# Moving slot distances from ScalarE to GpSimd, and one more layer-1 bias from TensorE to ScalarE, in a graph-network kernel

## The chip, the cores and the metric

One core of one Trainium2 chip. The metric is device microseconds of one execution. Engines are called as in the profile: PE is TensorE, PEld its weight loads, DVE is VectorE, ACT is ScalarE, POOL is GpSimd.

## The reference

A message-passing layer on 128 graphs of 64 nodes with 128 features. Every adjacent pair of nodes goes through a three-layer perceptron with a layernorm after each of the first two layers; the messages are summed per node, and an update perceptron of the same form follows.

```python
f_i = broadcast(part_feats[:, :, None, :]); f_j = broadcast(part_feats[:, None, :, :])
messages = _mlp(concatenate([f_i, f_j], -1), msg_w0, ... msg_b2)    # relu, LN, relu, LN, linear
messages = messages * coupling_matrix[..., None]
agg = sum(messages, axis=2)
updated = part_feats + _mlp(concatenate([part_feats, agg], -1), upd_w0, ... upd_b2)
```

The adjacency is sparse (about 1 in 8 and the diagonal), so the kernel computes only the edges that exist.

## The kernel before

Edges are packed into slots, 640 for each graph, so 1280 for a pair of graphs. Two pairs make a quad, with 5 chunks of 512 edges; four pairs make a block, with ten chunks. There are 160 chunks in 16 blocks. A loop over chunks issues work by a hand-made plan: `at(n, place, f, ...)` puts a call into iteration n at one of the places "a", "m", "b", "k", "x", "e" and some more. The plan fixes the order of instructions on every engine. Layer 1 of a chunk runs 8 iterations (L1) after its layer 0.

```python
def place(b):                       # where a block's edges lie among the slots, on POOL
    before = adp.tile([P, PB], F32, name="before")
    nc.gpsimd.tensor_tensor(before, cum, blk["deg"], op=ALU.subtract)
    blk["mid"] = adp.tile([P, PB], F32, name="mid")
    nc.gpsimd.tensor_tensor(blk["mid"], cum, before, op=ALU.add)
    ...
def distance(p):                    # ACT: distance of every slot from the middle of each node's slots
    D[p] = tpp.tile([P, CAP], F16, name="d", bufs=2)
    nc.scalar.activation(D[p], slot, AF.Abs, bias=blocks[b]["mid"][:, q:q + 1], scale=-1.0)

def make_tp(p):                     # DVE: 1 where the slot belongs to the node
    ...
    nc.vector.tensor_scalar(tp, D.pop(p), blocks[b]["deg"][:, q:q + 1], None, op0=ALU.is_lt)
...
def seed(n):                        # ACT puts the scaled bias into the PSUM bank of layer 1
    ...
    for t in range(CH):
        nc.scalar.activation(Z[n][:, t, :], W["b1b"], AF.Copy, scale=SR[q][:, k:k + 1])

def layer1(n):
    ...
    if n not in SEEDED:             # otherwise PE does it, with one matmul of 512 columns
        nc.tensor.matmul(ps, lhsT=SD[q], rhs=W["b1t"][:, CH * c:CH * c + CH, :], start=True, ...)
    for t in range(CH):
        nc.tensor.matmul(ps[:, t, :], lhsT=h[:, t * P:(t + 1) * P], rhs=W["w1c"], ...)
    nc.scalar.activation(Y[n], ps, AF.Relu)
...
for n in range(2, NCHK - L1):       # seven of ten chunks get the bias from ACT
    if n % CPB in (0, 1, 2, 6, 7, 9) or (n > CPB and n % CPB == 5):
        at(n + L1 - 2, "x", seed, n)
```

The bias has to be scaled by the layernorm's root of each edge. POOL computes the variance of a quad, ACT takes the root and splits it (sh), PE turns it (`ma<-ident,sh`), and ACT copies it out (sdT) for the bias matmuls of PE. For a chunk, the bias costs either PE one matmul or ACT four small copies.

## Time and profile before

| | before |
|---|---|
| median of 3 executions | 574.55 us (572.53 to 574.66) |
| span of the profiled execution | 569.1 us |
| start of the first layer 1 | 33.2 us |
| start of layer 1 of blocks 1, 2, 14, 15 (counted from 0) | 61.0, 92.6, 484.5, 520.0 us |
| one block in the middle | 32.65 us |
| bias: chunks by ACT, by PE | 104, 56 |

The block starts are read from the order of time on PE, as the start of the first layer-1 matmul of chunks 10, 20 and so on. In the text "interval 7" is the time from layer 1 of a chunk with number 7 in its block to layer 1 of the next one. The bias matmul of chunk 8, if it has one, lies at the end of interval 7. A block's length is the sum of the ten median intervals.

Two more views of the kernel before matter later. First, what PE's weight loads waited for from 200 to 500 us (total us, times, longest us):

```profile
PEld z L605 <- issue: 2.7, 16, 0.2
...
PEld hT L544 <- DVE st L548: 1.8, 8, 0.2
PEld z L605 <- ACT z L593: 0.3, 2, 0.2
```

No wait is longer than 0.2 us (the view leaves out waits of up to 0.15 us). Second, ACT's order of time in intervals 7 and 8 (start, duration, engine, line, operation, tiles):

```profile
245.64 0.70 ACT L538 ACTIVATE h<-hps,b0c 128x512 f32<-128x512 f32 x1
246.42 0.59 ACT L741 COPY ysumT<-ma 128x512 f32<-128x512 f32 x1
246.91 0.83 ACT L478 ACTIVATE d<-slot,mid 128x640 f16<-128x640 f16 x1
247.64 0.30 ACT L269 ACTIVATE m_sq<-m_v,eps_c 128x20 f32<-128x20 f32 x1
```

Remember the order: the copy of ysumT, which gives PE its PSUM bank "ma" back, comes straight after the relu h, and one of the distances stands behind it.

### The profile page before, as it was taken

The numbers are of one execution on the slowest core, as the hardware profiler recorded it, in microseconds if no ns is written. First come the engines' busy times: TensorE is split into PE (matmuls) and PEld (weight loads), VectorE is DVE, ScalarE is ACT, GpSimd is POOL, SyncE is SP. The second block draws the span as 40 slices with busy tenths as digits, with TensorE's granted clock in tenths as the row PEclk, the third lists the DMA queues.
The fourth block names the chain that finished last, engine by engine and source line by source line (L and its number), as shares of the span: only waits on it lengthen the run. The fifth ranks groups of instructions, "written<-read, shape, count | busy, mean of one in ns | idle before, by whom it ended". The sixth has DMA issues, their size and how long they took to land. (4 is left out here: it accounts for less than half of the span.)

```text
span 569.1 us, 15800 instructions
## 1 busy us (share of the span) xinstructions
PE 547.2 (96%) x5325; PEld 513.5 (90%) x5325; DVE 483.0 (85%) x1944; ACT 481.2 (85%) x1153; POOL 353.2 (62%) x911
## 2 busy tenths in 40 slices
PE   8799899999999999999999999999999999989894
PEld 7597889999999999999999999999999999979883
DVE  6768788998979899898989899898989989886685
ACT  6778989998989899898989899898989989885534
POOL 3535466766757676675758676675767666545452
PEclk9999999999999999999999999999999999999998
DMA  4475647354654745654556545647554545452101
GB/s 102 112 149 123 126 114 135 84 133 112 120 138 113 143 98 147 109 121 113 126 137 117 143 97 132 113 106 152 119 137 84 135 111 106 114 94 29 39 20 42
DMA packets 90770, 63.23 MB, mean 111 GB/s; under 512 B 57398, under 2 KB 74812, under 8 KB 90684
## 3 DMA queue, kind: packets, MB, share of 16 engines
q1 hardware_dynamic: 90396, 62.03, 49.8%
q8 instruction: 44, 0.72, 0.6%
q14 instruction: 42, 0.34, 0.2%
q10 hardware_dynamic: 288, 0.13, 0.1%
HBM read 6.82 MB, written 4.19 MB: 19 GB/s over the span
## 5 line engine op out<-in xcount | busy, mean ns | idle before, releaser
L605 PE MATMUL z<-w1c,h 128*128 128x128 f32 x1280 | 172.8, 278 | 0.0
L605 PEld LDWEIGHTS z<-w1c,h 128*128 128x128 f32 x1280 | 161.2, 192 | 7.7 <-issue 4.6
L548 DVE BATCH_NORM_STATS2 st<-hT 128x6 f32<-128x128 f32 x640 | 140.8, 281 | 30.3 <-PE hT L544 30.2
L593 ACT ACTIVATE z<-b1b,m_sd 128x128 f32<-128x128 f32 x416 | 154.3, 371 | 10.1
L615 DVE BATCH_NORM_STATS2 st<-y 128x6 f32<-128x128 f32 x640 | 137.3, 275 | 2.7 <-POOL m_d L245 1.3
L608 ACT ACTIVATE y<-z 128x512 f32<-128x512 f32 x160 | 94.4, 591 | 22.5 <-PE z L605 20.8
L538 ACT ACTIVATE h<-hps,b0c 128x512 f32<-128x512 f32 x160 | 109.5, 685 | 1.7 <-PE hps L535 1.6
L544 PE MATMUL hT<-ident,h 128*128 128x128 f32 x640 | 97.1, 274 | 1.8 <-DVE st L548 1.6
L678 POOL TENSOR_TENSOR w<-oh,m_q 128x320 f32<-128x320 f16 x126 | 92.1, 744 | 9.9 <-PE hT L544 5.3
L535 PE MATMUL hps<-s,abl 128*128 128x512 f32 (+3 forms) x256 | 91.8, 370 | 2.5 <-ACT h L538 2.0
L544 PEld LDWEIGHTS hT<-ident,h 128*128 128x128 f32 x640 | 74.7, 140 | 13.8 <-DVE st L548 4.6
L535 PE MATMUL hps<-s,abh 128*128 128x512 f32 (+3 forms) x256 | 78.3, 324 | 0.0
L691 PE MATMUL ys<-y,w 128*64 128x128 f32 x1280 | 76.9, 275 | 0.0
L691 PEld LDWEIGHTS ys<-y,w 128*64 128x64 f32 x1280 | 69.2, 137 | 4.2 <-issue 3.6
L245 POOL TENSOR_TENSOR m_d<-st 128x20 f32<-128x20 f32 x62 | 16.4, 264 | 80.6 <-DVE st L548 69.0
L517 DVE TENSOR_TENSOR j<-mk,cmpt 128x320 fp32r<-128x320 f32 x124 | 58.4, 471 | 1.2 <-PE mk L509 1.2
L493 POOL CAST i<-tp 128x640 fp32r<-128x640 f16 x58 | 41.7, 719 | 23.3 <-DVE tp L484 7.4
L478 ACT ACTIVATE d<-slot,mid 128x640 f16<-128x640 f16 x64 | 52.7, 824 | 0.0
L535 PEld LDWEIGHTS hps<-s,abl 128*128 128x128 f32 x256 | 49.1, 192 | 3.7 <-ACT h L538 2.7
L535 PEld LDWEIGHTS hps<-s,abh 128*128 128x128 f32 x256 | 49.2, 192 | 0.0
L469 DVE TENSOR_TENSOR abl<-mu,abh 128x512 fp32r<-128x512 f32 (+1 forms) x33 | 22.0, 667 | 30.3 <-ACT abh L463 30.2
L509 PE MATMUL mk<-tp,posall 128*128 128x320 f16 x126 | 37.7, 299 | 0.0
(227 smaller groups left out, 980.4 us busy)
## 6 DMA issues: line engine op xcount, KB each, us to landing
s<-i SPq DMA_DIRECT2D x124, 160.0 KB, 2.6
s<-j SPq DMA_DIRECT2D x124, 160.0 KB, 2.6
xn<-in_x_dram SPq DMA_DIRECT2D x15, 256.0 KB, 3.7
out_dram<-uo SPq DMA_DIRECT2D x15, 256.0 KB, 2.4
an<-in_adj_dram SPq DMA_DIRECT2D x16, 128.0 KB, 2.7
oh<-tp SPq DMA_TRANSPOSE x64, 3.3
xn<-in_x_dram SPq DMA_DIRECT2D x2, 128.0 KB
out_dram<-uo SPq DMA_DIRECT2D x2, 128.0 KB, 2.6
```

What stands on the lines that cost most here:

```text
L478: nc.scalar.activation(D[p], slot, AF.Abs, bias=blocks[b]["mid"][:, q:q + 1], scale=-1.0)
L517: nc.vector.tensor_tensor(JR[p][:, c], MK.pop((p, k))[:, 0:HC], cmpt[:, c], op=ALU.is_equal)
L535: nc.tensor.matmul(ps[:, c:c + w], lhsT=ab[:, g % 4, :], rhs=s, start=(k == 0), stop=(k == 1))
L538: nc.scalar.activation(H[n], ps, AF.Relu, bias=b0c)
L544: nc.tensor.transpose(ps[:, t, :], H[n][:, t * P:(t + 1) * P], ident)
L548: nc.vector.bn_stats(ST0[q][:, CH * c + t, :], ps[:, t, :])
L593: nc.scalar.activation(Z[n][:, t, :], W["b1b"], AF.Copy, scale=SR[q][:, k:k + 1])
L605: nc.tensor.matmul(ps[:, t, :], lhsT=h[:, t * P:(t + 1) * P], rhs=W["w1c"], start=False, stop=True, skip_group_check=True)
L608: nc.scalar.activation(Y[n], ps, AF.Relu)
L615: nc.vector.bn_stats(ST1[q][:, CH * c + t, :], Y[n][:, t, :])
L678: (nc.vector if p == NP - 2 else nc.gpsimd).tensor_tensor(WT[p][:, :, g, :], OH[p][:, :, g * N:(g + 1) * N], Q[q][:, k:k + TG].unsqueeze(2 ...
L691: nc.tensor.matmul(YS[b][g * N:(g + 1) * N, k, :], lhsT=w[:, t, g, :], rhs=y, start=(t == 0), stop=(t == TG - 1))
```

## The change

The intent is to use POOL, which is the least busy engine, for the distances, and to spend the ACT time that this frees on an eighth bias in ten, so that PE has less to do. On POOL the distance is a linear map, slot x scale + shift, written as a 16-bit float whose steps at 1536 are 1, so that the slots of a node all round to 1536 exactly; the comparison becomes "equal to 1536". Block 0 keeps ACT. Besides, the start is reordered: the bias table and the variance of the first quad change places, the second half of the first row terms goes to another PSUM bank, and nine small matmuls (keep_busy) are added to PE's work in the start.

```diff
@@ place(b)
-            blk["mid"] = adp.tile([P, PB], F32, name="mid")
-            nc.gpsimd.tensor_tensor(blk["mid"], cum, before, op=ALU.add)
+            half = adp.tile([P, PB], F32, name="half")
+            nc.vector.tensor_scalar(half, blk["deg"], 0.5, 2.0, op0=ALU.max, op1=ALU.mult)
+            blk["scale"] = adp.tile([P, PB], F32, name="scale")
+            nc.vector.reciprocal(blk["scale"], half)
+            mid = adp.tile([P, PB], F32, name="mid")
+            nc.gpsimd.tensor_tensor(mid, cum, before, op=ALU.add)
+            nc.gpsimd.tensor_tensor(mid, mid, blk["scale"], op=ALU.mult)
+            blk["shift"] = adp.tile([P, PB], F32, name="shift")
+            nc.gpsimd.tensor_scalar(blk["shift"], mid, -1.0, TIE, op0=ALU.mult, op1=ALU.add)
@@ rows(b, half)
-            ps = blk["ab_ps", half] if k0 else ubank()
+            ps = blk["ab_ps", half] if k0 else abank() if (b, half) == (0, 1) else ubank()
@@ distance(p), for b > 0
-            nc.scalar.activation(D[p], slot, AF.Abs, bias=blocks[b]["mid"][:, q:q + 1], scale=-1.0)
+            nc.gpsimd.tensor_scalar(D[p], slot, blocks[b]["scale"][:, q:q + 1],
+                                    blocks[b]["shift"][:, q:q + 1], op0=ALU.mult, op1=ALU.add)
@@ make_tp(p), for b > 0
-            nc.vector.tensor_scalar(tp, D.pop(p), blocks[b]["deg"][:, q:q + 1], None, op0=ALU.is_lt)
+                nc.vector.tensor_scalar(tp, D.pop(p), TIE, None, op0=ALU.is_equal)
@@ plan
-                    at(max(n - 7, p - 2), "a", distance, p)
+                    at(max(n - 7, p - 2), "x" if p == PB + 1 else "a", distance, p)
-                at(n - 5, "a", node_rows, p)
+                at(n - 5, "x" if p == PB else "a", node_rows, p)
-            at(n, "e0", var0_of, q)
+            at(3 if q == 0 else n, "x" if q == 0 else "e0", var0_of, q)
-            if n % CPB in (0, 1, 2, 6, 7, 9) or (n > CPB and n % CPB == 5):
+            if n % CPB in (0, 1, 2, 6, 7, 9) or (n > CPB and n % CPB in (5, 8)):
                 at(n + L1 - 2, "x", seed, n)
-        at(3, "b", bias_table)
+        at(3, "e", bias_table)
+        for n, k in ((2, 2), (3, 3), (4, 2), (5, 2)):
+            at(n, "e", keep_busy, k)
```

## The prediction

> **What bounds the kernel now.** I read the page first for the engines' shares, then the table of stretches, the order of time on TensorE (PE), the waits of PE, and last the groups and the order of time on GpSimd (POOL).
>
> ```profile
> PE 547.2 (96%) x5325; PEld 513.5 (90%) x5325; DVE 483.0 (85%) x1944; ACT 481.2 (85%) x1153; POOL 353.2 (62%) x911
> ```
>
> ```profile
> core 0: us, PE busy (x) PEld busy (x) DVE busy (x) ACT busy (x) POOL busy (x), PEclk, DMA share, GB/s
> 20.00:40.00 20.00, 17.00 (x136) 14.48 (x136) 13.36 (x46) 14.87 (x40) 11.12 (x18) 1.00 0.72 152
> ...
> 200.00:250.00 50.00, 50.00 (x500) 47.60 (x499) 45.56 (x188) 45.50 (x108) 34.34 (x92) 1.00 0.55 122
> 250.00:300.00 50.00, 50.00 (x502) 47.80 (x502) 44.07 (x178) 44.70 (x109) 33.23 (x84) 1.00 0.50 124
> ```
>
> The average hides three stages. From about 65 to 500 us PE never stops; ACT and DVE are busy about 90%, POOL 68%. In the first 65 us and the last 65 us PE has holes. A busy PE need not be one at its limit, because matmuls overlap and their ends are modelled, so I looked for a second sign: the same instruction one block (ten chunks of 512 edges) later. The turn of the layer-0 roots (L568) starts at 203.64 and again at 236.29, so a block takes 32.65 us; from the starts of layer 1 over thirteen blocks, nearly every chunk repeats within 0.02 us from block to block. An engine that waited on others would not repeat like that. So the middle is bound by what PE is given to do: 14 blocks x 32.65 = 457 us of the 569.
>
> The order of time on PE shows what one bias matmul (L602) costs. Columns: start, duration, engine, line, operation, operands, shapes, count.
>
> ```profile
> 213.14 0.60 PE L736 MATMUL ma<-ident,ysum 128*128 128x128 f32 x4
> 213.58 1.06 PE L605 MATMUL z<-w1c,h 128*128 128x128 f32 x8
> ...
> 215.51 0.60 PE L736 MATMUL ma<-ident,uy 128*128 128x128 f32 x4
> 215.87 0.48 PE L602 MATMUL z<-b1t,sdT 80*128 80x512 f32 x1
> 216.18 1.05 PE L605 MATMUL z<-w1c,h 128*128 128x128 f32 x8
> ```
>
> The same four transposes stand ahead of layer 1 twice: without the bias matmul layer 1 starts 0.44 us after them, with it 0.67 us. It costs 0.23 us of PE's stream, not its 0.48 us of duration.
>
> The start is another matter. The waits of PE in the first 70 us:
>
> ```profile
> PE ma L568 <- POOL sh L563: 2.3, 2, 1.5
> PE hps L535 <- ACT h L538: 2.0, 2, 1.6
> PE mu L180 <- DVE abl L469: 1.4, 1, 1.4
> ```
>
> The reader sees 5.7 us in which PE stood, of which 1.4 us come from a PSUM bank that the second half of the row terms held, and 1.6 us from ScalarE (ACT) reaching a relu late.
>
> **What the Trainium skill says.** "VectorE: DVE Perf Modes", section on the TRN2 errata, gives a matmul max(60, 6 + columns) cycles at 2.4 GHz: 518 cycles, 216 ns for 512 columns. The 0.23 us above agree. "ScalarE: Activation LUTs", section "What ACT_TABLE_LOAD costs", gives an ACTIVATE with a pointer operand 280 ns + 0.833 ns per element: 813 ns for 640 (the trace: 826) and 387 ns for 128 (the trace: 371). "GPSIMD Engine Reference", section 4.1, calls one-input operations on GpSimd roughly line-rate[...]; the cast below agrees (719 ns for 640), the tensor_scalar with a pointer doesn't obviously (about 620 ns for 128). "SBUF — State Buffer", section "Who interferes with whom", says that a VectorE (DVE) operation in a two-port mode and a GpSimd operation block each other whole; the trace agrees, since the slot comparison (L484) takes 0.36 us in most cases and about 1.01 us once in four, when a GpSimd operation runs.
>
> **The change part by part.** The groups that carry the costs:
>
> ```profile
> L478 ACT ACTIVATE d<-slot,mid 128x640 f16<-128x640 f16 x64 | 52.7, 824 | 0.0
> L593 ACT ACTIVATE z<-b1b,m_sd 128x128 f32<-128x128 f32 x416 | 154.3, 371 | 10.1
> L493 POOL CAST i<-tp 128x640 fp32r<-128x640 f16 x58 | 41.7, 719 | 23.3 <-DVE tp L484 7.4 <-ACT y L608 7.0 <-POOL posall L393 6.0
> L602 PE MATMUL z<-b1t,sdT 80*128 80x512 f32 x56 | 27.2, 486 | 0.0
> L646 POOL TENSOR_SCALAR b1lo<-b1lo,part 128x128 f32<-128x128 f32 x1 | 0.6, 622 | 0.1
> ```
>
> The two instruction orders, set against each other, give the counts.
>
> *Distances.* 60 of 64 leave ACT and become GpSimd tensor_scalars with two operations and two pointers. ACT loses 60 x 0.824 = 49.4 us, 3.3 us a block. What one costs on GpSimd is the weakest number here. At the cast's rate it is 0.72 us. The one tensor_scalar with a pointer in the trace took 0.62 us for 128 elements; if all above a fixed 0.2 us (operations of 4 elements take that) is per element, 640 take 2.3 us; if the excess is fixed, 1.04. I choose 1.3 us. GpSimd then gets 4 x 1.3 + 0.4 (two 4-element operations) = 5.6 us a block on top of 22.1 (67.6 us in 100 us, over the 32.65): 27.7 of 32.4, 85%. It isn't the bound. DVE gets two small operations a block, some 0.3 us.
>
> *Bias by ACT.* 14 bias matmuls go, 56 ACT copies of 0.371 come: 1.5 us more a block on ACT. With the distances gone ACT falls from 29.5 us a block to 29.5 - 3.3 + 1.5 = 27.7. PE saves 14 x 0.23 = 3.2 us, and in the middle all of it is on the path: the block should become 32.42 us. ACT's relief itself buys nothing there, because PE hardly waits for ACT.
>
> *Start.* The second half of the row terms takes another bank, and the first variance goes ahead of four table operations (0.46 + 0.62 + 0.62 + 0.45 = 2.2 us on GpSimd), in whose shadow ACT stood 1.8 us before the root. A distance (1.3 us) now stands there instead, so the variance gains about 0.9 us, and ACT is also rid of a cast (moved) and a distance ahead of the late relu: 0.7 + 0.8 us. Against that, nine warming matmuls of about 0.22 us enter PE, 2.0 us in all, placed in the holes. The bank's wait of 1.4 us shrinks to 0.7, since the next layer-0 matmul needs the same row terms anyway. The relu's 1.6 us should go. But the distance of the sixth pair now comes behind the first table part on GpSimd, at about 28.8 us, and its comparison on DVE can't run before that: DVE's next statistics start hardly earlier than the 29.55 us of before. I count 1.0 us of gain.
>
> Sum: 574.55 - 3.2 - 1.0 = 570.3 us. The end (500 us on) is not touched.
>
> **The rivals.**
>
> *GpSimd becomes a link that PE waits for.* The variance of a quad runs on GpSimd, goes to ACT, comes back and is turned by PE. GpSimd's slack ahead of it:
>
> ```profile
> 233.76 0.25 POOL L245 TENSOR_TENSOR m_d<-st 128x20 f32<-128x20 f32 x1 [1.78 <-DVE st L548]
> ...
> 249.19 0.25 POOL L245 TENSOR_TENSOR m_d<-st 128x20 f32<-128x20 f32 x1 [2.56 <-DVE st L548]
> ```
>
> One distance falls into the first gap, two into the second, where GpSimd works through from 233.76 to 246.6 with half a microsecond of rest. At 1.3 us each (2.6 in 2.56) they just fit. At 1.8 us the second variance is 1.0 us late, and PE's turn of the roots, which has at most 0.4 us of slack, waits perhaps 0.5 us a block: 14 x 0.5 = 7 us, about 577 us. At 2.3 us GpSimd has 31.6 of 32.4 us a block to do and each gap is missed: 1 us or more a block, 584 us or more. For it: the 622 ns of the lone tensor_scalar. Against: the cast's 719 ns for the same 640 elements.
>
> *The start gives more.* If the relu's wait goes and nothing catches up, 2 to 3 us instead of 1.0, and with 3.2 in the middle 568 us. If ACT's relief also removes the waits for the roots (2.3 us), 566. Against: those stand behind GpSimd, not ACT.
>
> *Nothing at the start, or a loss.* The warming matmuls (2.0 us) fill holes that no longer exist, and the late comparison holds DVE: 571 to 573 us.
>
> *Collisions.* Four more GpSimd operations a block meet DVE's two-port comparisons. A comparison lengthened by 0.65 us costs DVE up to 2.6 us of its 3 us of slack a block. The distance stands one chunk ahead of its own comparison, so few should meet; I give it no more than 0.5 us on average, inside the range.
>
> **Range and chances.** The certain term is 3.2 us of PE work; the others reach from +3 to -7 us or so. I take 570.3 us, 565.5 to 576.5. Over 2% faster needs 563.1 us or less, 11.5 us, when the visible removable PE time is 3.2 + 5.7: 0.03. Over 2% slower needs 586 us, which only the slowest GpSimd case gives: 0.04. Within: 0.93.
>
> **What would show it.** Right: 42 bias matmuls in place of 56; a block of 32.42 us with chunks repeating as exactly as before; PE busy throughout from 65 to 500; the distance at 1.0 to 1.5 us on GpSimd, GpSimd near 80% in the middle; ACT near 85%; layer 1 starting about 1 us before its 33.2 us of now. Wrong: a distance of 1.8 us or more with PE waiting for sh (L563's successor), or DVE waiting for d ahead of the comparison; a block of 32.65 us or longer; or a start shorter by 2 us or more.

## The result and the profile after

The changed kernel is slower: 581.59 us in the median of 4 executions (579.91 to 583.24), the kernel before 573.54 in the same rounds (570.91 to 574.66). A ratio here is the mean time of one kernel's runs over that of the other's of the same rounds, so not quite the ratio of the medians: 1.0147, interval 1.0098 to 1.0196. That is 1.5% slower, and above the range of the prediction (565.5 to 576.5), though in the class within 2% that it favoured; it had expected 0.7% less time, so the sign was wrong. The profiled spans are 569.1 and 579.5 us.

From the page after, engines and granted clock in 40 slices:

```profile
PE 554.1 (96%) x5329; PEld 513.5 (89%) x5329; DVE 487.0 (84%) x1974; ACT 458.0 (79%) x1149; POOL 410.8 (71%) x1001
...
PEclk9989999999999999999999999999999999998998
```

PE is busy for 6.9 us longer although it has less to do, ACT has lost 23 us and POOL gained 58. The groups after (busy us, mean ns):

```profile
L612 ACT ACTIVATE z<-b1b,m_sd 128x128 f32<-128x128 f32 x472 | 175.4, 372 | 11.5
...
L493 POOL TENSOR_SCALAR d<-slot,scale,shift 128x640 f16<-128x640 f16 x60 | 58.0, 966 | 0.1
```

The 56 new copies (472 for 416) and the 60 distances are there. A distance takes 0.97 us on POOL, less than the 1.3 us predicted, so the strongest rival of the prediction, a POOL that is too slow, is not the cause by itself. The table of stretches after:

```profile
20.00:40.00 20.00, 16.79 (x126) 14.57 (x125) 9.91 (x33) 10.24 (x29) 13.85 (x23) 0.91 0.61 127
...
200.00:250.00 50.00, 49.86 (x507) 46.58 (x502) 43.51 (x179) 40.59 (x103) 38.94 (x94) 1.00 0.60 114
```

Two things differ from before. In the first row the granted clock is 0.91 for 1.00, and DVE and ACT do a quarter to a third less. In the middle PE is no longer full, and ACT rests more.

**Where the 10.4 us went.** From the starts of layer 1:

| | before | after | difference |
|---|---|---|---|
| first layer 1 | 33.2 | 35.1 | +1.9 |
| layer 1 of block 1 | 61.0 | 64.3 | +3.3 |
| block 1 to block 15 | 459.0 | 466.0 | +7.0 |
| block 15 to the end | 49.1 | 49.2 | +0.1 |
| one block in the middle | 32.65 | 33.11 | +0.46 |

So a third of the loss is in the start and two thirds in the middle. In the middle three intervals of ten differ by more than 0.01 us: interval 5 takes 5.50 us for 5.31, interval 7 takes 2.65 for 2.61, although its bias matmul is gone, and interval 8 takes 4.20 for 3.94. Thirteen blocks of 0.46 make 6.0 of the 7.0 us. Most of the rest lies in block 14, where PE waits once for ysumT, the turned message sums: 1.9 us before, 3.0 after. All six kernels with chunk 8's bias on ACT show 3.0 there, the other six 1.9. What the weight loads waited for from 200 to 500 us, after:

```profile
PEld ma L755 <- ACT ysumT L760: 3.3, 9, 0.4
...
PEld ma L587 <- POOL sh L582: 2.3, 9, 0.3
```

Two waits are new, each once a block: for ACT's ysumT and for sh, the split root of the layernorm. ACT's order of time shows the first (L557 is the relu h, L612 the new bias copies, L760 ysumT), that of PE's weight loads shows what it does to PE:

```profile
251.44 0.70 ACT L557 ACTIVATE h<-hps,b0c 128x512 f32<-128x512 f32 x1
252.01 1.60 ACT L612 ACTIVATE z<-b1b,m_sd 128x128 f32<-128x128 f32 x4
253.56 0.58 ACT L760 COPY ysumT<-ma 128x512 f32<-128x512 f32 x1
254.03 0.31 ACT L270 ACTIVATE m_sq<-m_v,eps_c 128x20 f32<-128x20 f32 x1
```

```profile
254.19 0.42 PEld L755 LDWEIGHTS ma<-ident,uy 128*128 128x128 f32 x4 [0.37 <-ACT ysumT L760]
...
258.74 0.12 PEld L587 LDWEIGHTS ma<-ident,sh 128*80 128x80 f32 x1 [0.26 <-POOL sh L582]
```

Before, ysumT began 0.78 us after h; now it begins 2.12 us after it, since the four copies for chunk 8 (1.60 us) stand between. The distance that has gone stood behind ysumT, so it leaves no room at this place. PE's weight load stands 0.37 us for the bank. The root of the next quad is late in turn, and the weight load of its turn stands another 0.26 us for sh. Two things make sh late in this trace: DVE stands 0.73 us for m_sq (0.32 before) ahead of the statistics, and at the end of the chain POOL stands 0.47 us (0.28 before) for the half of sh that ACT itself copies.

**The start.** POOL's first work for block 1, DVE's comparison and PE's transposes, in order of time after:

```profile
20.92 0.20 POOL L389 TENSOR_TENSOR mid<-mid,scale 128x4 f32<-128x4 f32 x1 [2.29 <-DVE scale L386]
...
29.73 0.87 POOL L493 TENSOR_SCALAR d<-slot,scale,shift 128x640 f16<-128x640 f16 x1
```

```profile
30.63 1.15 DVE L504 TENSOR_SCALAR tp<-d 128x640 f16<-128x640 f16 x1 [3.66 <-POOL d L493]
```

```profile
32.83 0.42 PEld L563 LDWEIGHTS hT<-ident,h 128*128 128x128 f32 x4 [2.28 <-DVE st L567]
```

POOL stands 2.29 us for the reciprocal of DVE. The distance of pair 5 comes behind the bias table, at 29.73. DVE stands 3.66 us for it, its statistics (st) come late, and PE's weight loads stand 2.28 us, PE itself 2.1. Then a second loss follows. Layer 1 of the first chunk after that gap, and the granted clock of the stretch behind it (the clock is the number before the last two):

```profile
35.14 1.91 PE L624 MATMUL z<-w1c,h 128*128 128x128 f32 x8
```

```profile
36.00:38.00 2.00, 2.00 (x10) 2.00 (x10) 0.00 (x0) 0.60 (x1) 0.00 (x0) 0.50 0.96 257
```

The eight matmuls take 1.91 us; in the kernel before the same took 1.05. The Trainium skill, "TensorE: Matmul & The Clock Gate", section "What's actually happening", says that TensorE's clock falls to half after an idle window and comes back after a busy one, and that the window runs freely. The trace agrees with the half: 0.50. It doesn't show that a whole window has to be idle: the gap here was 2.1 us (see the last section).

**Clock and spread.** The kernels e4, e5 and e6 below are the same program up to layer 1 of block 1, and in each PE has one gap of 1.4 us near 30 us. In their profiles 6.8 us, 3.4 us and nothing at half clock follow, and block 1 starts at 63.7, 62.7 and 61.0. So 3.4 us at half clock went with a loss of 1.7 us, 6.8 us with one of 2.7, and whether they come differs between executions of the same code. Most of the spread of the times goes with the clock too. Of the fourteen executions of the kernel before in the last two series of experiments, the seven with a mean clock of 0.994 or 0.995 took 570.3 to 571.1 us, the six with 0.989 took 572.0 to 574.7. The changed kernel took 579.91 at 0.994. At like clock it is 9 us slower, so the loss is not a matter of the clock alone.

### The profile page after: what moved, and what is told of

Read it like the earlier page. It is cut to its first block, busy times and chain, and to the rows that moved or that the text cites. A ratio compares the mean times of both kernels' runs of the same rounds, so it can differ in the third digit from the quotient of the medians.

```text
span 579.5 us, 15960 instructions
## 1 busy us (share of the span) xinstructions
PE 554.1 (96%) x5329; PEld 513.5 (89%) x5329; DVE 487.0 (84%) x1974; ACT 458.0 (79%) x1149; POOL 410.8 (71%) x1001
## 5 line engine op out<-in xcount | busy, mean ns | idle before, releaser
L612 ACT ACTIVATE z<-b1b,m_sd 128x128 f32<-128x128 f32 x472 | 175.4, 372 | 11.5
L557 ACT ACTIVATE h<-hps,b0c 128x512 f32<-128x512 f32 x160 | 109.3, 683 | 1.3 <-PE hps L554 1.3
L493 POOL TENSOR_SCALAR d<-slot,scale,shift 128x640 f16<-128x640 f16 x60 | 58.0, 966 | 0.1
L478 DVE TENSOR_TENSOR abl<-mu,abh 128x512 fp32r<-128x512 f32 (+1 forms) x32 | 21.3, 666 | 29.7 <-ACT abh L472 29.5
L472 ACT CAST abh<-mu 128x512 fp32r<-128x512 f32 (+1 forms) x32 | 18.3, 571 | 34.8 <-PE mu L460 34.8
```

The source lines that it names most:

```text
L493: nc.gpsimd.tensor_scalar(D[p], slot, blocks[b]["scale"][:, q:q + 1], blocks[b]["shift"][:, q:q + 1], op0=ALU.mult, op1=ALU.add)
L557: nc.scalar.activation(H[n], ps, AF.Relu, bias=b0c)
```

## The experiments

The theory from the traces has three parts: (A) in the middle, the four bias copies are put where ACT has no room; (B) in the middle, the two small operations for scale stand on DVE ahead of the update's layer norm, where DVE has no room; (C) in the start, distances of block 1 come too late on POOL. The rival is that POOL's distances as such, by collisions with DVE or by POOL's load, cost the time. Ten kernels ran, all gave correct results, in three series, each with its own runs of the kernel before. "After" below is the changed kernel. Mind the names in the expectations: there "Theory A" and "A2" mean part A, but "Theory B" and "B2" mean the rival and not part B.

**e1_bias_only.** The kernel before with nothing but the eighth bias:

```diff
-  (n > CPB and n % CPB == 5)
+  (n > CPB and n % CPB in (5, 8))
```

> The kernel before plus only the eighth ScalarE bias of ten chunks; distances stay on ScalarE. Blocks are measured from the start of layer 1 in one chunk to that ten chunks later, in the middle (before 32.65 us, after 33.11). Theory A (the four new bias copies stand on ScalarE ahead of the copy of the message sums and of the layer-1 root, and PE waits for what comes behind them): a block of 33.2 us or more, since the distance stays behind the copies too; 580 us or more in all. Theory B (GpSimd's distances are what PE waits for): a block of 32.4 us and about 570 us, as my prediction had it for this part.

Measured: 586.48 us, before 572.47, ratio 1.0230 (1.0191 to 1.0269). A block takes 33.65 us, with interval 8 at 4.92, as Theory A expected (33.2 or more). Without the relief from the distances, ACT's copies cost still more, and PE also waits for the relu h:

```profile
PEld hps L535 <- ACT h L538: 5.6, 9, 0.6
...
PEld ma L568 <- POOL sh L563: 2.5, 9, 0.3
```

The wait for sh is there without any distance on POOL, so ACT's lateness is enough to make it.

**e2_dist_only.** After without the eighth bias:

```diff
-  (n > CPB and n % CPB in (5, 8))
+  (n > CPB and n % CPB == 5)
```

> The changed kernel without the eighth bias on ScalarE (the bias matmul is back); distances on GpSimd, start as changed. Theory A: the waits for the message sums' turn and for the roots' turn go, a block is 32.65 plus the 0.18 us of the statistics' wait, 32.8 us; the start still costs 3.7 us; 579 us in all. Theory B: the waits stay and PE has 0.23 us more to do, a block of 33.1 to 33.3 us, 582 us or more.

Measured: 577.12 us, before 572.47, ratio 1.0054 (0.9995 to 1.0113). A block takes 32.78 us (Theory A: 32.8, the rival: 33.1 or more); intervals 7 and 8 are back at 2.60 and 3.93, and interval 5 stays at 5.50. So the eighth bias costs 33.11 - 32.78 = 0.33 us a block where 0.23 should have been saved: part A. Counting ACT's busy time in one block of this trace, I find 1.14 us of idle time in interval 5, but 0.12, 0.21 and 0.14 in intervals 6 to 8, where the new copies go. They take 1.60. The relief is real, and it lies elsewhere. The start was worse here (first layer 1 at 36.9 us), with the same waits as after and a longer stretch of half clock.

**e3_seed_late.** After with the copies for chunk 8 one place later, behind ysumT and m_sq:

```diff
-  at(n + L1 - 2, "x", seed, n)
+  if n > CPB and n % CPB == 8:
+      at(n + L1 - 1, "a", seed, n)
+  else:
+      at(n + L1 - 2, "x", seed, n)
```

> The changed kernel with the eighth bias emitted one place later on ScalarE, behind the copy of the message sums and the layer-1 root. Nothing else differs. Theory A: both waits (0.27 and 0.26 us a block) go, a block of about 32.6 us, 574.5 us in all. Theory B: a block stays at 33.1, 581.5 us.

Measured: 584.45 us, before 572.47, ratio 1.0190 (1.0138 to 1.0242); a block takes 33.30 us. Two of the four executions had the clock at 0.995 and took 582.4, two had 0.984 to 0.986 and took 586.5 and 586.7. The waits from 200 to 500 us:

```profile
PEld ma L587 <- POOL sh L582: 2.5, 9, 0.3
PEld z L624 <- ACT z L612: 2.1, 9, 0.2
```

The wait for ysumT is gone, and layer 1 now waits for its bias instead. Interval 7 gains (2.52), interval 8 loses (4.52). Both expectations (32.6 and 33.1) missed. The wait for sh stays although m_sq now comes early; in this trace POOL stands 1.13 us for ACT's half of sh. So this other order of ACT's work only moves the wait, which fits a stretch with more work for ACT than time.

**e4_scale_early.** After, with half and reciprocal out of place(b), planned two iterations earlier (the expectation says three) where DVE has room, for block 1 right behind its ranks, and taken from the last rank instead of ACT's copy of it:

```diff
+  def scales(b):
+      nc.vector.tensor_scalar(half, blk["rk"][:, :, N - 1], 0.5, 2.0, op0=ALU.max, op1=ALU.mult)
+      nc.vector.reciprocal(blk["scale"], half)
   def place(b):
-      (the same two operations)
```

> The changed kernel with the two new VectorE operations (half and scale) made from the ranks, three iterations earlier, in a place where VectorE stands idle (first block: right behind the ranks). If these two cause the 0.18 us wait of the transposes for VectorE's statistics, a block falls to 32.93 us; in the start GpSimd no longer waits 2.3 us for scale, its first distance comes 2 us earlier and layer 1 starts at about 33 us instead of 35.1: 577 us in all. If the wait comes from comparisons that collide with GpSimd, the block stays at 33.1 and only the start gains: 579.5 us.

Measured: 578.72 us, before 572.47, ratio 1.0080 (1.0027 to 1.0133). A block takes 32.94 us, interval 5 is back at 5.31, and nothing else moved: part B, 0.17 us a block, as expected. In the start DVE stands 1.73 us for pair 5's distance instead of 3.66, yet layer 1 starts at 34.2, not at the 33 expected, in a stretch of half clock. This is what stood there after, on DVE:

```profile
243.07 0.15 DVE L384 TENSOR_SCALAR half<-deg 128x4 f32<-128x4 f32 x1
243.25 0.18 DVE L386 RECIPROCAL scale<-half 128x4 f32<-128x4 f32 x1
243.35 0.66 DVE L239 CUSTOM_DVE_ANT_0 uy<-mu,usdb 128x512 f32<-128x512 f32 x1
```

In the kernel before, DVE is idle for only 0.03 to 0.04 us in each of intervals 4 and 5, so 0.28 us ahead of uy goes straight into the statistics that PE's next transposes wait for.

**e5_seed4.** As e4, with the eighth bias in chunk 4 in place of chunk 8:

```diff
-  (n > CPB and n % CPB in (5, 8))
+  (n > CPB and n % CPB in (4, 5))
```

> The kernel of e4 (scale early), but of ten chunks the fourth-numbered (n mod 10 = 4) and not the eighth has its bias from ScalarE; as many copies, as many matmuls saved. Theory A2 (ScalarE has no slack in the chunks numbered 6 to 9 of a block: in the changed kernel it stands idle 0.1 us of each, but 0.7 us in each of the chunks 2 and 3): both waits go and the saved matmul counts, a block of 32.94 - 0.27 - 0.26 = 32.4 us; about 32.4/32.94 of e4 in the middle, 571 us in all with the slow start. Theory B2 (any additional bias copy, or GpSimd's later variance, costs as much as the matmul saves, wherever it stands): 32.7 us or more.

Measured: 570.29 us, before 571.10, ratio 0.9973 (0.9916 to 1.0029); a block takes 32.57 us. The waits for ysumT and sh are gone. Same work, other place, 0.37 us a block less than e4: this settles part A. But the gain is small: the block misses the expected 32.4, and the interval of the ratio includes 1. Interval 3, which loses the matmul, falls only from 3.28 to 3.13, and interval 5 rises from 5.31 to 5.41, so 0.05 remain of the 0.23. The order of time says where the rest went. In interval 3 the weight load for the turn of the root starts 2.99 us after layer 1 instead of 2.82, just after sh, which now ends at 2.94 instead of 2.76. In interval 5 the weight load of the next layer 0 starts at 0.88 instead of 0.78, just after ACT's relu h, which ends at 0.83 instead of 0.52. (These are medians over blocks 3 to 13, against e4.) Even the good place makes ACT a little late, by less than the wait view lists.

**e6_no_turn.** As e4, with the turn of the root, and the small operations that prepare it, left out for the odd quads 3 to 29, all of whose biases come from ACT (cut):

```diff
-  at(..., turn_root, q); at(..., root_out, q)
+  if not (q % 2 and 1 < q < NQ - 1):
+      at(..., turn_root, q); at(..., root_out, q)
```

> The kernel of e4 (scale early, eighth bias as changed), without the turn of the roots of those odd quads in which every chunk now has its bias from ScalarE: PE's turn, two small ScalarE copies and a GpSimd subtraction, whose results nothing reads. If PE's wait for that turn costs 0.23 us a block besides the turn's 0.11, the block falls from 32.94 to 32.6 us and 574 us in all; if the wait only moves to the next instruction that hangs on the late ScalarE, it falls by 0.11 to 0.2 us.

Measured: 574.39 us, before 571.10, ratio 1.0042 (0.9994 to 1.0091); a block takes 32.85 us, 0.09 less than e4. I had meant to remove the wait for sh, and missed: the turn that waits in interval 8 is that of the even quads, which still need it, while the one left out ran in interval 3 (3.27 to 3.16).

Both waits of after stay as they were (ysumT 3.3 us, sh 2.3 us in 300). What the run does show is the price of a turn, about 0.1 us. That the time met the 574 us of the first expectation is luck: its block of 32.6 us did not come, and the profile has no half clock in the start, where e4's has 6.8 us of it.

**e7_act_block1.** After, with the distances of block 1 on ACT as before (place(b) then makes mid and no scale for it):

```diff
-  if b == 0:      # distance, make_tp
+  if b <= 1:
```

> The changed kernel with the distances of the second block (pairs 4 to 7) back on ScalarE; the rest of the start (bank, warming matmuls, order of variance and table) as changed, the middle as changed. If the start's loss comes from GpSimd's distances of that block (waiting for scale, standing behind the bias table, and holding VectorE's comparison for 3.7 us), layer 1 starts at 32 to 33 us instead of 35 to 37 and the time is 578 us; if it comes from the warming matmuls and the new order, layer 1 still starts at 35 us or later, 581.5 us.

Measured: 576.48 us, before 571.10, ratio 1.0075 (1.0027 to 1.0124). The first layer 1 starts at 32.0 us instead of 35.1, and block 1 at 59.6 instead of 64.3; the middle is that of after (33.11). The waits of PE in the first 70 us, with "DVE st" at 2.9 in total and 2.1 at most in the kernel after:

```profile
PE ma L591 <- POOL sh L586: 2.2, 2, 1.4
...
PE hT L567 <- DVE st L571: 0.9, 3, 0.4
```

The eight matmuls of the first layer 1 take 1.05 us again, and the clock from 20 to 40 us is 1.00. This shows part C: four distances on POOL cost the start 4.7 us, 3.1 by the first layer 1 and 1.6 behind it, where the half clock had been. The clock is not chance alone: the profiles of after, e2 and e3, which share their start, all have half clock there (first layer 1 at 35.1 to 37.0), those of e7 to e10, with block 1 on ACT, have none (32.0 to 32.5). The rest of the new start is a gain: 59.6 is 1.4 us earlier than the kernel before.

**e8_best1.** All remedies together: scale early, eighth bias in chunk 4, block 1 on ACT (the edits of e4, e5 and e7; block 1 then needs no scale).

> Scale early, chunk 4 in place of 8 for the bias on ScalarE, and the second block's distances on ScalarE, together. Theory A2 and the start's cause as in e7: a block of 32.4 us, layer 1 from 32.5 us on, 569 us in all, 0.6% below the kernel before. Otherwise at or above the kernel before.

Measured: 567.73 us, before 571.10, ratio 0.9927 (0.9877 to 0.9976). This is the lowest median. From 200 to 250 us PE is full again:

```profile
200.00:250.00 50.00, 50.00 (x499) 47.50 (x498) 45.50 (x189) 44.44 (x112) 41.33 (x104) 1.00 0.59 119
```

A block takes 32.57 us (32.4 was expected), block 1 starts at 60.1.

**e9_nine.** As e8, with chunk 3 as a ninth chunk by ACT, and no turn for the even quads, which then don't need it:

```diff
-  (n > CPB and n % CPB in (4, 5))
+  (n > CPB and n % CPB in (3, 4, 5))
```

> e8 with one more bias on ScalarE (chunks 3 and 4, so nine of ten; chunk 8 stays a matmul), and without the turn of the even quads' roots, which nothing then reads. PE has 0.23 + 0.11 us less to do a block. If ScalarE's slack in chunks 0 to 3 (3.2 us a block in the changed kernel, of which the copies for chunk 4 took 1.5) carries it: a block of 32.2 us, 563.5 us in all. If ScalarE is by then the bound of that stretch: 32.5 us or more, 568 us or more.

Measured: 579.95 us, before 571.82, ratio 1.0139 (1.0107 to 1.0172). A block takes 33.42 us. Interval 2 loses its matmul and falls from 2.62 to 2.38, interval 8 loses its turn (3.94 to 3.82), but interval 3 rises from 3.13 to 4.33. In e8 ACT had 0.46 us of idle time in interval 2 and 0.10 each in 3 and 4, and the copies take 1.6. PE now waits for another copy of ACT:

```profile
PEld mu L777 <- ACT uhT L768: 7.9, 9, 0.9
```

The mechanism of part A at another place, with another victim: the second branch of the expectation, but with a block longer by 0.9 us than its "32.5 us or more".

**e10_dist_early.** e8 without the eighth bias: the distances alone, put well.

```diff
-  (n > CPB and n % CPB in (4, 5))
+  (n > CPB and n % CPB == 5)
```

> Distances on GpSimd alone (second block's on ScalarE, scale early), the eighth bias as a matmul, as before the change. ScalarE has 3.3 us a block less to do than before, PE the same. If PE bounds the middle, as I had it, a block takes the 32.65 us of before (32.6 to 32.7); only the start differs: 571.5 us in all, 1 us below before. If ScalarE's relief is worth something by itself, a block of 32.4 us or less and 568 us.

Measured: 568.68 us, before 571.82, ratio 0.9947 (0.9919 to 0.9976); a block takes 32.60 us, as before (32.65). So 56 distances on POOL cost the middle nothing, and buy it nothing: the rival falls. Collisions did become more frequent: 27 of the 64 slot comparisons took over 0.6 us, against 15 before, and it did no harm to the block. Of the 33.11 us after, 32.60 are the kernel with distances, 32.94 - 32.60 = 0.34 the eighth bias in the wrong place (0.33 by e2), and 33.11 - 32.94 = 0.17 the scale in the wrong place (0.18 by e2). They add up.

What the eighth bias is worth in e8: 568.68 and 567.73 us come from different series, and at the same clock of 0.997 the two took 568.1 and 567.5 to 567.8. That is about half a microsecond, and the executions overlap: one of e10 took 567.7 at 0.995. Their profiles differ by 1.2 us, yet that is nearly all one event: in both, PE stands 1.9 us for ysumT in block 14, and then layer 1 runs at the half clock in e10 and not in e8. First e10, then e8:

```profile
510.37 1.91 PE L630 MATMUL z<-w1c,h 128*128 128x128 f32 x8
```

```profile
510.00 1.05 PE L630 MATMUL z<-w1c,h 128*128 128x128 f32 x8
```

The wait itself is there in the kernel before too. That its consequence depends on how the gap falls in the clock's window would fit the page cited above; no run shows the cause. For the same reason the 0.73% of e8 over the kernel before is partly clock: at 0.995 the one took 569.0, the other 570.6 to 571.1 in the same series.

## Why the prediction was wrong

**"An engine that waited on others would not repeat like that."** On this the prediction rests its claim that the middle is bound by PE's work alone. The sign doesn't hold: in e1 and after, where PE waits for ACT in every block, each interval from block 3 to 13 also repeats within 0.02 us. (The reading that PE never stops from 65 us on also misses a gap of 1.1 us at 73.)

**"In the middle all of it is on the path: the block should become 32.42 us."** This step failed. The size of the saving was right: interval 2 of e9 falls by 0.24 us for one bias matmul. What failed is the assumption that PE would wait for nothing in its place. The block became 33.11, not 32.42; without the eighth bias (e2) it is 32.78, so the bias costs 0.33 us where it should have saved 0.23.

**"ACT falls from 29.5 us a block to ... 27.7. ACT's relief itself buys nothing there."** The sum of the block was the wrong measure. ACT fell nearly as counted, to 28.1 us a block, but the time came free in intervals 0, 2 and 5 (idle 1.10, 0.13 and 0.19 us before, 1.55, 0.73 and 1.14 after) and the new work went to intervals 6 to 8, where ACT had a tenth of a microsecond idle in each. The prediction even read that PE "hardly waits for ACT" and took it as room; it only says that ACT was in time, by how much it doesn't say.

**"DVE gets two small operations a block, some 0.3 us."** The size was right (0.28), but it was entered at no cost. It cost 0.17 to 0.18 us a block, 2.5 us over 14 blocks.

**"I count 1.0 us of gain" at the start.** Without block 1's distances on POOL the start gains 1.4 us (e7), so the sum of the terms for bank, variance, relu and warming matmuls was about right; no run measures them singly. The late comparison, which the prediction saw ("can't run before that"), was taken to cost DVE's statistics nothing; it cost PE 2.1 us, and 1.6 us more were lost behind it, where the clock was at half. The rival "nothing at the start, or a loss" named it and put it at 571 to 573 us, too small, because neither POOL's wait for the reciprocal nor the clock was in it.

**A distance of 1.3 us on POOL** was too high (0.875 us median, 0.97 mean), and yet the rival built on slow distances (577 us at 1.8 us each, 584 at 2.3) gave times on both sides of the measured 581.59, with the very wait it named, PE waiting for sh. That is luck, for its reason was wrong: e1 has that wait with all distances on ACT, e10 has none of it with the distances on POOL.

**Right:** 42 bias matmuls, POOL near 80% in the middle (38.94 of 50 us; the prediction's own sum had given 85%), no cost of collisions in the middle (e10), and the end untouched (+0.1 us).

What stays open: what decides whether a gap of PE is followed by the half clock in a given execution, and how the late sh of after divides between DVE's wait for m_sq and ACT's own copy.

## What to carry to other kernels

Room on an engine is to be looked up at the place in its order where the new work goes, per interval and not per block: of two versions with the same eight biases, one with the new copies where ACT had room and one with them elsewhere, a block differed by 0.37 us, more than the whole expected gain. A small operation is not free when it stands on a full engine ahead of a step that others wait for: 0.28 us on DVE cost 0.17 us a block. That an order repeats exactly from block to block does not show that its engine waits for nothing. In the start, a producer moved to another engine should be checked against everything queued ahead of it there, and a PE gap of 1.4 to 2.1 us should be priced at more than its length, since here up to 1.7 us came on top with each 3.4 us of half clock.

## What the Trainium skill lacked or had wrong

- "TensorE: Matmul & The Clock Gate", section "HAM oscillation — how this bites in real kernels", gives the rule to avoid gaps of more than about 3.4 us on PE. Here a gap of 2.1 us was followed by a clock of 0.50, and eight matmuls in 1.91 us for 1.05. A gap of 1.9 us was followed by the half clock in e10 and not in e8, one of 1.4 us in e5 and not in e6.
- "GPSIMD Engine Reference", section 4.1, says of the cost of one-input operations only that they are roughly line-rate. A tensor_scalar with two pointers on 128x640 f16 took 0.875 us in the median (0.860 to 1.332) and one of 4 elements 0.20 us, so some 1.05 ns an element on top of 0.2 us.
